# A two-layer Mamba and ternary-FFN kernel: one Strassen sum moved into PSUM, the last step of both layer norms moved from VectorE to ScalarE, and a new priority table

## Chip, cores and metric

The kernel runs on one core of one Trainium2 chip. The metric is the device time of one execution in microseconds (us), as a median of several executions, of the kernel before and of the changed one. Lower is better. The engines are called as in the profile: PE (TensorE matmul), PEld (its weight load), DVE (VectorE), ACT (ScalarE), POOL (GpSimd), SP (SyncE, which issues all the data transfers here).

## What is computed

Input `u` is 2 x 2048 x 512 in fp32. A Mamba-2 layer and a feed-forward layer with ternary weights follow one another, and after each of them the input of the layer is added and the sum is normalised over its 512 columns (post-LN). Cut to what matters here:

```python
def _layernorm(x, eps=1e-05):
    m = jnp.mean(x, axis=-1, keepdims=True)
    v = jnp.var(x, axis=-1, keepdims=True)
    return (x - m) / jnp.sqrt(v + eps)

# attention layer (a selective state space layer), then
x = _layernorm(u + mamba(u))

# feed-forward layer, W_up and W_gate 2048 x 512, W_down 512 x 2048
scale = jnp.mean(jnp.abs(w)) + EPS                       # for each of the three weights
q = jnp.clip(jnp.round(w / scale), -1.0, 1.0) * scale    # ternary weight
h = silu(x @ W_gate.T) * (x @ W_up.T)                    # the ternary weights
y = h @ W_down.T
out = _layernorm(x + y)
```

Which of the two first weights gets the SiLU is a matter of how the kernel stores them and changes nothing below: one half of the Strassen outputs (`c11`, `a2`) goes through SiLU, the other half (`c12`, `c22`) is multiplied by it.

## The kernel before, in words

**Two stages that overlap at one seam.** The first stage is the Mamba layer: 16 groups of 256 positions (`proj`, `steps`, `scan`), each with projections on PE (the lines 616 and 633), a convolution on ACT and DVE (638 and 640), a scan, and an output projection (833) whose operands go through two transposing transfers (824 and 826). While it runs, the weights of the second stage are read twice and made ternary. Results go to `s_scratch` in DRAM. The second stage is the feed-forward layer: 8 blocks of 512 rows (`FSTART`, the loop at 962), and the text below calls them blocks 0 to 7.

**One block of the second stage.** For each of its four chunks of 128 rows: load (`Fs`, `Fu`), add the input (`Fa`, line 970), statistics on DVE (`Fb`, 973 to 975), the power -1/2 on POOL (`Fp`, 977), and then the normalisation itself, `(x - mean) * rstd`, as one DVE instruction over 128x512 (`Fn`, line 978). Then sums of quarters of the block for Strassen's form (`FS`, 991), a split into a high and a low fp16 part (`Fh`, `Fl`, 996 and 997) and a transposing transfer (`FT`, 999). Then eight *pairs* (`pair(p, ...)`, line 920), each for 256 of the 2048 hidden columns. Then, for each chunk, the down projection (`Fd`, 1010, four steps of eight matmuls of 128x512), the residual (`Fr`, 1014), statistics (`Fe`, 1017 to 1019), the power on POOL (`Fq`, 1021), the normalisation on DVE (`Fm`, line 1022) and the store (`Fo`, 1023).

**One pair.** Seven products P1 to P7 (line 932, eight matmuls of 128x256 each) in three PSUM banks, `A`, `Bk` and `Ck`. Bank `A` gathers P1, then P6, then P7, then P4, and after each of the first three ACT copies the sum reached so far to SBUF (`k1` to `p1`, `k2` to `u2`, `k3` to `u3`, all line 936). Bank `Bk` holds P2 alone, and DVE adds the copy to it (`c11` = P2 + `p1`, line 937). Bank `Ck` holds P5, to which DVE adds `u3` (`c22`), then P3 on top of P5, to which DVE adds `u2` (`c12`). ACT takes SiLU of `c11` in place (`a1`, 951) and of bank `A` (`a2`, 952). DVE multiplies (`g`, 956), and `h` on ACT (957) and `l` on DVE (958) split the product into fp16 parts, which are the operands of the down projection.

**Banks.** The kind `fA` has two banks (shared before with `sd`), `fB` two (shared with `tr` and `sd`), `fC` two (shared with `mm`). So a third pair's P2 needs the first pair's `Bk` back, and so on.

**Order.** Nothing is ordered by hand. Each step is recorded with `op(name, engine, cost, function, r=, w=)`. `Order.run` then plays the whole program through with the given costs: each engine takes, of the steps that are ready and have their buffers, the one with the smallest key, and the order found this way is emitted, engine by engine. The keys come from the dictionary `TABLE` (lines 38 to 203), one number per step name, with `name@0` for the first group or block alone. So the order on all five queues follows from the costs and the table. `Var`s read or written in the planner become semaphore waits in the program. 80 filler steps of four matmuls on a matrix of ones (line 572) have no table entry, and so they go where the planner's PE has nothing else to do.

Of the kernel before, what the change touches and what calls it, by code (L numbers as in the profile page):

```python
# [11 lines left out]
F16 = mybir.dt.float16  # L12
AF = mybir.ActivationFunctionType
ALU = mybir.AluOpType
# [24 lines left out]
    "Fh1.3@0": -880.0, "xe4@0": -833.42, "xs3@0": -798.3, "Fr1@0": -749.32, "x1@0": -743.53, "Fk2.4@0": -708.12,  # L39
    "t10@0": -702.07, "FT0@0": -701.5, "Fh0.1@0": -696.72, "x0@0": -647.64, "t00@0": -647.63, "e@0": -617.3, "Fl1.5@0":  # L40
    -611.36, "xg@0": -606.03, "uspw@0": -605.28, "Fl0.4@0": -604.72, "Fl6@0": -595.97, "Fl1.1@0": -595.59, "Fd33@0":
    -577.19, "Fo1@0": -575.43, "Fl0.0@0": -559.34, "Fo2@0": -542.58, "FP6.4@0": -515.99, "Fu0@0": -510.53, "Fg0.6@0":
    -496.82, "Fk1.1@0": -495.69, "Fa1.3@0": -493.84, "Fa2.4@0": -491.28, "Fu1@0": -489.5, "Fa1.0@0": -468.24, "FP4.1@0":
    -464.74, "FT4@0": -443.92, "Fo0@0": -443.36, "t71@0": -441.8, "Fk1.5@0": -434.25, "FP7.3@0": -433.72, "FS5@0":
    -424.07, "Fk3.4@0": -410.98, "sz11@0": -409.89, "t41@0": -408.76, "Fc22.5@0": -403.36, "FS4@0": -400.51, "Fc11.5@0":
    -399.71, "yh.1": -396.1, "B111": -393.2, "wb7ld": -392.43, "xf@0": -390.09, "Fa1.2@0": -389.2, "sg01@0": -387.76,
    "Fk2.1@0": -378.9, "md1.0": -370.41, "Fa1.0": -363.95, "Fl1.7@0": -354.48, "w.1@0": -354.31, "Fk3.2@0": -340.52,
    "Fh0.3@0": -335.11, "Fc22.6@0": -333.55, "Fh1.5@0": -330.02, "Fk3.6@0": -329.97, "sg00": -329.64, "Fk1.2@0":
    -325.88, "Fl0.2@0": -323.01, "Fk3.1@0": -321.43, "Fd12@0": -320.02, "Fe1@0": -318.37, "Fh0.6@0": -316.51, "nA0":
    -314.95, "xe5@0": -313.85, "sz10": -313.05, "Fa1.5@0": -310.03, "FP7.1@0": -305.86, "Fk3.0@0": -305.34, "Fk2.6@0":  # L50
    -304.93, "Fl0.0": -302.95, "yh.0@0": -290.81, "cst@0": -290.24, "ssq.0@0": -289.03, "q2@0": -288.45, "Fc12.4@0":
    -287.51, "q_9@0": -286.63, "Fh0.1": -286.35, "z02@0": -284.82, "x3@0": -283.55, "Fk3.2": -283.16, "xt4@0": -280.75,
    "Fk1.5": -280.01, "Fd10@0": -277.81, "ulo@0": -275.56, "Fh1@0": -272.36, "FP7.5@0": -269.7, "Fd13@0": -269.26,
    "FP3.1@0": -268.96, "Fg0.1@0": -268.88, "wx1hi": -268.5, "Fk1.1": -265.49, "md0.1@0": -265.29, "yg0.1": -259.58,
    "T26": -257.61, "sz11": -256.09, "Fk3.1": -252.55, "wx3sq": -249.32, "Fl0.7@0": -247.92, "cs0@0": -247.82,
    "Fa2.1@0": -245.85, "Fc11.3@0": -245.84, "t72@0": -244.74, "t33": -240.45, "Fk1.7@0": -240.2, "rl@0": -240.04,
    "FP6.1@0": -239.95, "ce.1@0": -239.95, "q1@0": -238.9, "v0": -238.05, "Fd01@0": -237.72, "xec0@0": -236.84,
    "Fa2.2@0": -236.43, "bte@0": -235.45, "FT4": -229.58, "t73@0": -229.2, "xs2": -229.13, "Fq2@0": -229.12, "Fp3@0":
    -228.34, "FP7.5": -227.33, "Fp0@0": -226.27, "Fg1.5": -225.08, "q3@0": -223.61, "t71": -223.59, "t12": -223.14,
    "Fh1.4@0": -223.12, "FP1.1@0": -221.59, "FP3.6@0": -221.11, "cr0": -220.95, "Fg1.5@0": -218.61, "Fh1.2@0": -218.5,  # L60
    "T17": -217.95, "cr1@0": -217.62, "yh.0": -216.95, "Fs2@0": -216.52, "sz02@0": -216.25, "ul@0": -216.02, "s.0@0":
    -215.43, "Fn3@0": -215.09, "xe": -214.89, "B220": -213.53, "Fr1": -210.21, "Fg0.2@0": -206.86, "ec0@0": -204.35,
    "t52": -204.15, "yg1.1@0": -204.07, "cst0": -203.33, "FP7.4@0": -201.23, "wz1rc": -200.8, "usq@0": -200.21,
    "sg00@0": -200.19, "Fe1": -199.59, "T25": -199.49, "szs2": -198.11, "b122": -197.76, "b121": -197.75, "Fd23@0":
    -197.61, "Fk1.2": -197.55, "FP6.6@0": -196.92, "z12@0": -196.48, "wx3rc": -196.43, "Fk3.5@0": -196.29, "xs6":
    -196.28, "q3": -195.54, "t40": -195.35, "sg10@0": -194.31, "wz2ld": -193.93, "xs2@0": -193.52, "st.1@0": -193.33,
    "Fl0.3@0": -192.79, "wb1ld": -192.61, "t42@0": -192.22, "Fa1.5": -192.04, "t82@0": -191.59, "wx1rc": -191.29,
    "m1.0@0": -190.47, "gm.0": -190.01, "yg1.1": -189.77, "o0.1": -189.76, "Fk1.6@0": -189.4, "xt4": -189.35, "xw0.0@0":
    -188.31, "T43": -188.06, "rs.1@0": -187.71, "xe5": -185.77, "wx0sq": -184.8, "wb5lo": -183.47, "t81@0": -182.69,
    "wx8rc": -182.68, "wz0rc": -182.67, "wz0sq": -182.2, "z02": -181.39, "Fc12.2@0": -181.07, "Fl6": -179.08, "t32":  # L70
    -178.42, "xt3": -177.5, "xt5@0": -175.63, "q4": -175.58, "Fk2.1": -174.34, "yd0.0@0": -173.37, "sz12": -172.32,
    "Fg1.7@0": -172.03, "Fc11.4@0": -171.73, "sg11@0": -171.14, "wd0": -168.11, "cs1@0": -166.86, "t80@0": -166.6,
    "cmm@0": -166.05, "wx2mm": -165.65, "Fc22.4@0": -165.51, "xe@0": -165.49, "Fo3@0": -165.02, "Fd03": -164.7, "FT2@0":
    -164.31, "yd1.0@0": -163.73, "x4": -163.52, "wx0mx": -163.51, "dm7": -162.69, "btr": -162.68, "ce.0": -162.14,
    "xt0": -160.74, "Fc12.2": -159.66, "Fc12.4": -159.1, "Fk1.3@0": -157.73, "btr@0": -157.68, "Fh0.3": -157.61, "T36":
    -157.33, "t01@0": -157.03, "Fo2": -156.36, "T15": -155.92, "t01": -155.89, "T20": -155.87, "T21": -155.05, "uspw":
    -155.0, "FP4.2": -154.58, "FT0": -153.73, "xs5@0": -152.56, "T23": -152.33, "wz1pw": -150.53, "Fl0.5": -146.77,
    "yh.1@0": -146.56, "md1.0@0": -146.53, "Fc11.7@0": -145.51, "wx2mx": -141.54, "xt7@0": -140.5, "Fl0.2": -140.44,
    "Fl1.0@0": -137.01, "Fh6@0": -136.3, "q0": -135.1, "wx1mm": -134.74, "Fg1.3@0": -134.09, "wa1ld": -132.88, "wz1sq":
    -131.2, "cs1": -130.62, "m0.0@0": -130.26, "x5@0": -129.87, "dec.1": -128.06, "Fg1.0": -126.87, "FP6.0@0": -126.78,  # L80
    "xe7": -126.54, "wb7hi": -126.27, "t61": -126.26, "Fq0@0": -126.0, "FP5.1@0": -125.85, "wz0mx": -125.2, "tl.0@0":
    -123.56, "FP4.0@0": -122.92, "xe2@0": -121.58, "Fl0.4": -121.56, "Fg0.2": -121.29, "FP4.2@0": -120.92, "x8@0":
    -120.84, "Fh1.0": -120.38, "Fc11.2@0": -120.35, "Fg0.7@0": -119.99, "t03@0": -119.65, "t51@0": -119.23, "t11":
    -119.08, "uh": -119.08, "Fh0@0": -118.27, "Fa2.1": -118.24, "e": -117.06, "Fh0.6": -116.27, "FP3.3": -115.89, "FT3":
    -115.77, "t13@0": -113.43, "Fh2": -112.97, "FP7.1": -112.51, "Fa1.7@0": -112.45, "Fg1.1@0": -112.14, "wx1sq":
    -111.85, "xt6@0": -111.31, "Fd33": -110.87, "yo.1": -109.95, "b120": -109.3, "wa2sq": -108.74, "t00": -108.46,
    "t21": -108.2, "wx8pw": -108.11, "Fk1.7": -107.55, "FP6.2@0": -106.84, "B210": -106.57, "wx8lo": -106.56, "wx8mx":
    -106.52, "t23@0": -105.54, "xt0@0": -105.51, "Fk3.6": -105.47, "wx3mm": -104.71, "Fa1.2": -104.62, "b125": -104.6,
    "uh@0": -104.09, "xs1@0": -103.96, "md1.1": -103.77, "szs0": -103.22, "Fl1@0": -103.22, "xw1.0@0": -103.14, "Fl0.1":
    -103.05, "Fk3.0": -102.44, "stc.0": -102.38, "Fk2.7": -102.36, "yg0.0": -102.3, "wz0lo": -102.2, "q6": -102.18,  # L90
    "t10": -102.16, "gm.1": -101.95, "wz2rc": -101.94, "t02": -101.82, "pw.0": -101.74, "Fk1.0@0": -101.67, "cmm":
    -101.45, "sz10@0": -101.11, "wa4ld": -100.89, "xec0": -99.7, "T14": -99.66, "Fc11.6@0": -99.48, "z00@0": -99.46,
    "wa7ld": -99.04, "wb1hi": -96.71, "cwu0": -96.62, "t63": -96.56, "T22": -96.55, "FP6.1": -95.56, "T11": -95.43,
    "Fa2.3@0": -92.55, "Fk3.4": -91.8, "sz01@0": -91.16, "Fd02@0": -90.79, "Fl0.5@0": -90.31, "Fl5@0": -89.42,
    "Fl1.2@0": -89.28, "Fn1@0": -89.22, "Fg1.4@0": -89.03, "t11@0": -88.61, "Fa1.4@0": -88.6, "cwx1": -88.44, "Fk2.3@0":
# [299 lines left out]
def mamba_ffn_kernel(  # L395
# [45 lines left out]
    with ExitStack() as ph:  # L441
# [478 lines left out]
        def pair(p, xT, hh_, hl_):  # L920
# [17 lines left out]
            prod("P1", 0, B11, A, True, False)  # L938
            copy("k1", p1, A)
            prod("P2", 1, B21, Bk, True, True)  # L940
            add("c11", c11, Bk, p1)
            prod("P6", 5, T2, A, False, False)
            copy("k2", u2, A)
            prod("P5", 4, T1, Ck, True, False)
# [128 lines left out]
```

## Time and profile before

| | us |
|---|---|
| median of 3 executions | 1398.83 (1398.15, 1398.83 and 1402.92) |
| the profiled execution | 1400.29 |
| its span (first to last instruction and transfer) | 1398.6 |
| PE busy | 1373.4 |
| DVE busy | 1141.8 |
| ACT busy | 858.7 |
| POOL busy | 85.8 |

The profile is of one execution. Its busy times are by engine, and "idle before" in a group of instructions is the time that the engine stood still just ahead of them, with what ended it. The mean ns of a matmul in a group is longer than its share of PE's time, since matmuls follow each other before the earlier has ended; how often they start is what counts. The granted TensorE clock of this execution is 0.999.

### The profile page before, as it was taken

The page shows a single profiled execution, that of the slowest core. Times are in us where ns is not written, and L with a number is a line of the kernel's source. Part 1 is how long each engine was busy: PE and PEld are TensorE (multiplying, and loading weights), DVE is VectorE, ACT ScalarE, POOL GpSimd, SP SyncE. Part 2 cuts the span into 40 slices and gives each one's busy share as a digit, 9 for nine tenths or more (in the row PEclk, how much of TensorE's full clock was granted, in tenths as well). Part 3 has the DMA queues.
Part 4 walks back from the last instruction along what each step waited for, and adds up shares of the span by engine and source line. Part 5 has one row for each costly group of instructions (what it writes and reads, how often), then busy time and mean ns, then how long its engine had stood idle before and what let it go on. Part 6 is the DMA issues. An engine that isn't in the chain of part 4 may idle for free.

```text
span 1398.6 us, 26861 instructions
## 1 busy us (share of the span) xinstructions
PE 1373.4 (98%) x10276; PEld 986.8 (71%) x10276; DVE 1141.8 (82%) x2903; ACT 858.7 (61%) x1539; POOL 85.8 (6%) x128
## 2 busy tenths in 40 slices
PE   9999999999999999999999999999999999999997
PEld 8767666766776666767676776868677777768684
DVE  5798898888798999999899766959687786959665
ACT  7778877788776665666677553636454453636351
POOL 1002001000000000000000000000010100000000
PEclk9999999999999999999999999999999999999999
DMA  5354465443444555366649422222222222221100
GB/s 204 108 167 129 114 167 144 145 137 99 133 114 130 135 151 145 86 157 163 140 118 226 129 39 68 53 69 65 57 84 61 76 53 81 49 83 39 46 9 31
DMA packets 186257, 147.04 MB, mean 105 GB/s; under 512 B 133904, under 2 KB 142352, under 8 KB 185872
## 3 DMA queue, kind: packets, MB, share of 16 engines
q1 hardware_dynamic: 186128, 145.33, 39.1%
q8 instruction: 80, 1.31, 0.4%
q14 instruction: 49, 0.40, 0.1%
HBM read 90.63 MB, written 23.20 MB: 81 GB/s over the span
## 4 chain that ended last, share of the span: by engine, by line
PE 49%; ACT 2%; DVE 2%; DMA 1%; issue 0%; POOL 0%; POOLq 0%; ACTq 0%; DVEq 0%
PE sd L932 18%; PE ms L1010 8%; PE mm L932 8%; PE po L1010 8%; PE po L833 2%; PE tr L932 2%; PE mm L616 1%; PE mm L633 1%; DMA th<-yh 1%; PE sd L813 1%; DVE acc L640 0%; DVE cr L806 0%; ACT L743 0%; ACT L644 0%; ACT L745 0%
## 5 line engine op out<-in xcount | busy, mean ns | idle before, releaser
L640 DVE SCALAR_TENSOR_TENSOR acc<-mm,cwu,acc 128x256 f32<-128x256 f32 x432 | 198.4, 474 | 24.1 <-ACT acc L638 22.6
L633 PEld LDWEIGHTS <-wx 128*128 128x128 f16 x1728 | 165.3, 97 | 37.9 <-issue 3.6
L633 PE MATMUL mm<-uh,wx 128*128 128x260 f16 x1152 | 152.5, 274 | 2.4 <-DVE acc L640 0.9
L616 PE MATMUL mm<-wz,uh 128*128 128x344 f16 x768 | 127.7, 309 | 5.1 <-DVE acc L640 3.4
L833 PE MATMUL po<-wo,th 128*128 128x512 f16 x512 | 121.0, 379 | 4.4 <-DMA th<-yh 4.2
L932 PEld LDWEIGHTS <-xt 128*128 128x128 f16 x1024 | 100.2, 98 | 20.4 <-issue 0.9
L957 ACT ACTIVATE sz<-y 128x512 f16<-128x512 f32 x128 | 80.5, 629 | 52.7 <-DVE y L956 40.8
L638 ACT ACTIVATE acc<-mm,cst,cwu 128x256 f32<-128x256 f32 x144 | 79.1, 557 | 53.9 <-PE mm L633 51.9
L932 PEld LDWEIGHTS <-wz 128*128 128x128 f16 x1024 | 100.2, 98 | 16.7
L932 PEld LDWEIGHTS <-wx 128*128 128x128 f16 x1024 | 100.1, 98 | 16.3
L616 PEld LDWEIGHTS <-uh 128*128 128x128 f16 x768 | 74.2, 98 | 41.9 <-issue 4.6
L958 DVE TENSOR_TENSOR cr<-y,sz 128x512 f16<-128x512 f32 x128 | 87.4, 684 | 17.3 <-ACT sz L957 16.5
L936 ACT ACTIVATE ec<-sd 128x512 f32<-128x512 f32 x97 | 57.3, 592 | 70.3 <-DVE y L937 33.3
L1010 PE MATMUL ms<-wo,sz 128*128 128x512 f16 x256 | 97.0, 379 | 0.0
L1010 PE MATMUL ms<-wo,cr 128*128 128x512 f16 x256 | 97.0, 379 | 0.0
L1010 PE MATMUL po<-wo,sz 128*128 128x512 f16 x256 | 97.0, 379 | 0.0
L1010 PE MATMUL po<-wo,cr 128*128 128x512 f16 x256 | 97.0, 379 | 0.0
L833 PEld LDWEIGHTS <-th 128*128 128x128 f16 x512 | 49.2, 98 | 54.6 <-DMA th<-yh 5.0
L633 PE MATMUL mm<-ul,wx 128*128 128x260 f16 x576 | 87.5, 273 | 0.0
L1010 PEld LDWEIGHTS <-cr 128*128 128x128 f16 x512 | 50.1, 98 | 50.5
L1010 PEld LDWEIGHTS <-sz 128*128 128x128 f16 x512 | 50.1, 98 | 50.5
L936 ACT ACTIVATE xw<-sd 128x512 f32<-128x512 f32 x63 | 37.5, 595 | 62.1 <-PE sd L932 33.3
(205 smaller groups left out, 2929.7 us busy)
## 6 DMA issues: line engine op xcount, KB each, us to landing
cr<-cum_scratch SPq DMA_DIRECT2D x32, 512.0 KB, 5.4
uraw<-in_uT_dram SPq DMA_DIRECT2D x16, 520.0 KB, 4.9
ec<-cum_scratch SPq DMA_DIRECT2D x64, 128.0 KB, 5.2
fraw<-in_wupT_dram SPq DMA_DIRECT2D x32, 256.0 KB, 3.1
s_scratch<-s SPq DMA_DIRECT2D x32, 256.0 KB, 2.4
x<-s_scratch SPq DMA_DIRECT2D x32, 256.0 KB, 2.8
fraw<-in_wgateT_dram SPq DMA_DIRECT2D x32, 256.0 KB, 2.9
fraw<-in_wdownT_dram SPq DMA_DIRECT2D x32, 256.0 KB, 3.4
```

Of the source, the lines that this page charges most:

```text
L616: T.matmul(ps[:, :ZC], (uh, ul)[a][:, k, HL + c * P:HL + (c + 1) * P], wz4[b]()[:, j, k, :], start=(n == 0), stop=(n == 11))
L633: T.matmul(ps[:, :TW], wx4[a]()[:, j, k, :], (uh, ul)[b][:, k, :], start=(n == 0), stop=(n == 11))
L638: op(f"t{j}3", "S", act(TG, 2), lambda: S.activation(acc.ap, ps[:, HL:TW], AF.Identity, bias=cb[:, j:j + 1], scale=cwu[:, j, 3:4]), r=[ps, ...
L640: op(f"t{j}{k}", "V", stt(TG), lambda k=k: V.scalar_tensor_tensor(acc.ap, ps[:, 1 + k:1 + k + TG], cwu[:, j, k:k + 1], acc.ap, ALU.mult, A ...
L813: T.matmul(yp[hf][:, i * P:(i + 1) * P], cr[:, h, :], xt[:, c, h, :], start=is_first(g, c), stop=(is_first(g, c) or i == 3))
L833: T.matmul(po.ap, t[:, k, :], wo3[b]()[:, k, :], start=(q == 0 and k == 0), stop=(q == 2 and k == 7))
L932: T.matmul(bank_[:, fi * TG:(fi + 1) * TG], wt[:, kt, f * P:(f + 1) * P], xT[i][:, a, :, kt, :], start=(first and fi == 0 and n == 0), sto ...
L936: copy = lambda nm, t, bank_: o(nm, "S", 0.52, lambda: S.activation(t.ap, bank_.ap, AF.Copy), r=[bank_], w=[t])
L957: o(f"h{t}", "S", 0.54, lambda g_=g_, hv=hv, hh_=hh_: S.activation(hv(hh_), two(g_), AF.Copy), r=[g_], w=[(hh_[p // 2], (p, t))])
L958: o(f"l{t}", "V", tt(512), lambda g_=g_, hv=hv, hh_=hh_, hl_=hl_: V.tensor_tensor(hv(hl_), two(g_), hv(hh_), ALU.subtract), r=[g_, (hh_[p ...
L1010: T.matmul(po.ap, h[qd][:, f, c * P:(c + 1) * P], wd[qd // 2][:, 4 * (qd % 2) + f, :], start=(qd == 0 and f == 0 and a == 0), stop=(qd == ...
```

## The change

Three edits, and a new table.

1. `k1` no longer writes the SBUF buffer `p1` but the bank `Bk` itself. P2 then runs without a start flag, so that it adds to what ACT has put there. The DVE step `c11` is gone, and the SiLU `a1` reads the bank. The buffer `fp1` goes to `fu2` as a third buffer. In block 0 the first two pairs get one more matmul each, `in` (128x512), ahead of `k1`, which starts the bank with any values, so that the later matmuls find the bank's elements written.
2. The normalisations `Fn` and `Fm` go from DVE to ACT, as one Identity activation with two pointer operands (scale and bias). DVE makes the bias, `-mean * rstd`, in a new 128x1 step (`Fz`, `Fy`).
3. P1, P2 and P5 each keep the order of the pairs among themselves (`turn`), and so do the copies `k1` (`turn_k1`).
4. `TABLE` has new numbers for all steps (319 changed lines, left out here). The planner's order of the first stage changes with it.

```diff
-                ("fp1", [on("ec", 0, 0, 2048)]), ("fu2", [on("ec", 1, 0, 2048), on("xw", 0, 0, 2048)]),
+                ("fu2", [on("ec", 1, 0, 2048), on("xw", 0, 0, 2048), on("ec", 0, 0, 2048)]),
...
+        turn = {nm: fixed() for nm in ("P1", "P2", "P5")}
+        turn_k1, oh = fixed(), ones.bitcast(F16)
-        def pair(p, xT, hh_, hl_):
+        def pair(b, p, xT, hh_, hl_):
...
-                o(nm, "PE", 8 * 0.109, mm, r=[xT[i], kf(wt, p)], w=[bank_])
+                o(nm, "PE", 8 * 0.109, mm, r=[xT[i], kf(wt, p)], w=[bank_] + ([turn[nm]] if nm in turn else []))
...
             prod("P1", 0, B11, A, True, False)
-            copy("k1", p1, A)
-            prod("P2", 1, B21, Bk, True, True)
-            add("c11", c11, Bk, p1)
+            if b == 0 and p < 2:
+                o("in", "PE", 0.22, lambda: T.matmul(Bk.ap, oh[:, :P], B11[:, 0, :DM], start=True, stop=True), r=[kf(B11, 0)], w=[Bk])
+            o("k1", "S", 0.52, lambda: S.activation(Bk.ap, A.ap, AF.Copy), r=[A], w=[Bk, turn_k1])
+            prod("P2", 1, B21, Bk, False, True)
...
-            o("a1", "S", silu(512, 1), lambda: S.activation(c11.ap, c11.ap, AF.Silu, scale=facs[:, 0:1]), r=[ksc], w=[c11], table="silu")
+            o("a1", "S", silu(512, 1), lambda: S.activation(c11.ap, Bk.ap, AF.Silu, scale=facs[:, 0:1]), r=[Bk, ksc], w=[c11], table="silu")
...
-                op(f"Fn{c}", "V", 0.46, lambda c=c, x1=x1, mv=mv, rs=rs: V.tensor_scalar(x1[:, c, :], x1[:, c, :], mv[:, 0:1], rs[:, 1:2], ALU.subtract, ALU.mult),
+                op(f"Fz{c}", "V", 0.08, lambda mv=mv, rs=rs: V.scalar_tensor_tensor(mv[:, 0:1], mv[:, 0:1], -1.0, rs[:, 1:2], ALU.mult, ALU.mult), r=[rs], w=[mv])
+                op(f"Fn{c}", "S", act(DM, 2), lambda c=c, x1=x1, mv=mv, rs=rs: S.activation(x1[:, c, :], x1[:, c, :], AF.Identity, bias=mv[:, 0:1], scale=rs[:, 1:2]),
                    r=[mv, rs], w=[(x1, c)])
...
-                op(f"Fm{c}", "V", 0.46, lambda r=r, mv=mv, rs=rs: V.tensor_scalar(r.ap, r.ap, mv[:, 0:1], rs[:, 1:2], ALU.subtract, ALU.mult), r=[mv, rs], w=[r])
+                op(f"Fy{c}", "V", 0.08, lambda mv=mv, rs=rs: V.scalar_tensor_tensor(mv[:, 0:1], mv[:, 0:1], -1.0, rs[:, 1:2], ALU.mult, ALU.mult), r=[rs], w=[mv])
+                op(f"Fm{c}", "S", act(DM, 2), lambda r=r, mv=mv, rs=rs: S.activation(r.ap, r.ap, AF.Identity, bias=mv[:, 0:1], scale=rs[:, 1:2]), r=[mv, rs], w=[r])
```

## The prediction

> **What bounds the kernel now.** First the page's top, then busy time in four stretches, then three blocks of the second stage by themselves, then PE's own waits, then the end. The first fence is the page's head.
>
> ```profile
> span 1398.6 us, 26861 instructions
> ...
> PE 1373.4 (98%) x10276; PEld 986.8 (71%) x10276; DVE 1141.8 (82%) x2903; ACT 858.7 (61%) x1539; POOL 85.8 (6%) x128
> ...
> PEclk9999999999999999999999999999999999999999
> ```
>
> PE is busy for 1373.4 of 1398.6 us at the full clock, so 25.2 us are all that a change which leaves the products alone can win. The next view, busy time by stretch (each column an engine, in brackets its instructions), tells where they lie.
>
> ```profile
> 0.00:100.00 100.00, 94.14 (x773) 75.28 (x774) 72.71 (x229) 76.15 (x142) 9.97 (x21) 1.00 0.51 159
> 100.00:800.00 700.00, 688.12 (x5094) 480.06 (x5092) 627.03 (x1892) 499.21 (x925) 40.54 (x51) 1.00 0.53 139
> 800.00:1392.00 592.00, 591.10 (x4413) 431.48 (x4411) 439.34 (x779) 283.30 (x474) 34.23 (x54) 1.00 0.22 56
> 1392.00:1398.60 6.60, 0.00 (x0) 0.00 (x0) 2.75 (x7) 0.00 (x0) 1.10 (x2) 0.85 0.21 79
> ```
>
> PE stands for 5.9 us in the first 100, 11.9 us in the rest of the first stage, 0.9 us in nearly all of the second stage, 6.6 us after the last matmul. The second stage is the one that edits 1 and 2 touch. Three of its blocks, in the same columns:
>
> ```profile
> 899.40:976.00 76.60, 76.60 (x579) 56.40 (x578) 59.46 (x109) 37.81 (x65) 5.08 (x8) 1.00 0.25 66
> 976.00:1052.60 76.60, 76.60 (x579) 56.42 (x577) 59.56 (x108) 37.87 (x65) 5.08 (x8) 1.00 0.25 66
> 1052.60:1129.20 76.60, 76.60 (x579) 56.42 (x578) 59.47 (x108) 37.80 (x64) 5.08 (x8) 1.00 0.25 66
> ```
>
> Each lasts 76.60 us and PE is busy for all of it. A block's matmuls alone make 8 pairs x 7 products x 0.873 us (eight matmuls that start every 0.109 us) + 16 down steps x 1.727 = 76.5 us. So a steady block can't get shorter by anything done to DVE (78% busy) or ACT (49%). PE's waits, longest first, show what the first stage's idle time waits for:
>
> ```profile
> PE po L833 <- DMA th<-yh: 4.2, 3, 1.6
> PE mm L616 <- DVE acc L640: 3.4, 4, 1.9
> PE tr L648 <- ACT xt L650: 2.0, 5, 0.7
> PE mm L616 <- DVE v L621: 1.5, 1, 1.5
> ```
>
> The largest is the transposing transfer `th`, three times, 1.2 to 1.6 us each. Last, the end, in order of time:
>
> ```profile
> 1391.97 0.75 DVE L1014 SCALAR_TENSOR_TENSOR s<-po,facs,x 128x512 f32<-128x512 f32 x1
> ...
> 1392.77 0.55 DVE L1022 TENSOR_SCALAR junk<-junk,mv,lnr 128x512 f32<-128x512 f32 x1
> 1393.23 0.69 DVE L1017 BATCH_NORM_STATS2 bst<-s 128x6 f32<-128x512 f32 x1
> ...
> 1395.05 0.55 DVE L1022 TENSOR_SCALAR s<-s,mv,lnr 128x512 f32<-128x512 f32 x1 [0.73 <-POOL lnr L1021]
> 1395.63 0.33 SPq L1023 DMA_DIRECT2D out_dram<-s  x1
> ```
>
> The last chunk's statistics stand behind the normalisation of the chunk before (`junk`), on DVE's queue.
>
> **The change, part by part.**
>
> *The sum `c11`.* 64 DVE adds of 0.686 us (line 937) go: 43.9 us of DVE, 5.5 in a block. On the path: nothing, since PE covers them. `k1` stays one ACT copy. No row has ACT writing PSUM. Reading PSUM instead of SBUF takes 35 ns off (592 against 627 ns, lines 936 and 996), so I bound the write to PSUM by 557 and 627 ns and take 592; over 64 copies that is 2.2 us of ACT either way. `a1` now reads PSUM as `a2` does: 685 for 718 ns, 2.1 us of ACT less.
>
> What is new is a wait: P2 now waits for `k1`, and with P2 everything behind it in PE's queue. I counted the PE work that stands between them in the order the changed program was emitted in. After P1, `k1` needs 0.16 (the last matmul's tail, 273 less 109 ns), 0.03 of hand-over, 0.59 and about 0.06 back: 0.84 us. In a steady block P1 to P2 has 1.75 us of other products once (pair 0) and 5.2 to 20.9 us in the other seven. P6 waited for `k1` before and still does. Short covers of 1.73 to 1.75 us, over P1-P2, P1-P6, P6-P7 and P7-P4, are 10 in a block before and 12 after, and the 10 cost nothing in the blocks shown. So I take 0, with 0.9 us of margin at each; if that is gone, each overrun costs its own length (a rival below). At the seam, pair 0 of block 0 has only one scan step of 0.9 us between P1 and P2: up to 0.1 us.
>
> The two `in` matmuls are PE work: 2 x 0.216 (a 512-wide matmul starts every 0.216 us at line 1010) = +0.43.
>
> The Trainium skill speaks against the seed: "PSUM — Partial Sum Buffer", "Summary: rules for kernel authors", says that a sum seeded by ACT or DVE must be seeded with 0, as these engines do not set the bits by which a matmul adds, and its section "The four PSUM rules" would send any other seed through PE. No row here shows those bits. By that advice a seed per pair would be 62 more `in` matmuls, +13.4 us; the diff issues two, so the sum has two.
>
> *The normalisations.* 32 `Fn` of 539 and 32 `Fm` of 544 ns leave DVE (34.7 us), and 64 steps on 128x1 come (166 ns, from the 128x16 step of line 698; bounds 153, line 975, and 222, line 621): 10.6 us. On ACT 64 activations with two pointers: without pointers 627 ns (line 996), and two pointers add 182 (line 638 with two takes 557 at 128x256, line 650 without 375): 0.81 us, so 51.8 us; bounds 0.63 (pointers free) and 0.90 (the one-pointer SiLU of line 951, 718 ns, and 182 more). A steady block then has DVE 59.5 - 5.5 - 4.3 + 1.3 = 51.0 and ACT 37.8 - 0.3 + 6.5 = 44.0 of 76.6 us. Both lie under PE. DVE gets 67.9 us lighter in all, and in the second stage no wait of PE's is there to get shorter. Behind `Fn` on ACT stand the splits `Fh` and copies, behind `Fo`, which now waits for ACT, SP's loads for the next block; both are covered by the 33 us of ACT's idle time in a block and by a block's lead of those loads, so 0, and at most 0.81 each on the last chunk, counted below. Of the 64, the eight `Fn` of the first two blocks fall into the first stage, 6.5 us on an ACT that is busy for 499 of 700 us. The third buffer `fu2` and the `turn` orders issue no instruction: 0.
>
> The Trainium skill says the same against the move: "ScalarE: Activation LUTs", "Rules for kernel authors", puts add and multiply on VectorE. The rows agree in sign, 0.54 on DVE against an estimated 0.81 on ACT. If ACT set the pace the move would cost 64 x 0.27 = 17 us; at 57% of a block it doesn't.
>
> *The end.* `Fm` on ACT is 0.81 for 0.55, behind a step of 0.17 and two hand-overs of 0.06 on the last chunk: +0.55. The last statistics now wait for a step of 0.17 instead of one of 0.55: -0.4. Together +0.15. In block 7 PE waits 0.74 us for `k3` (its longest wait for line 936): before, P4 of pair 7 stands directly behind P7; in the new order two other products stand between: -0.74.
>
> *The table.* It moves the first stage, where 17.8 us of idle PE lie. Filler steps and products open in nearly the same order in both programs (15, 6, 7 and 3 fillers between the same four small matmuls), so I leave the first 100 us alone: 0, bounds -5.9 (its whole idle time) and +5.9. ACT loads its tables 76 times for 74, 2 x 1.28 us on an engine 71% busy there: 0. For `th` I counted again. From the scan's last product to the output projection a chunk needs 0.68 (815) + 1.24 (820) + 0.15 + 0.73 (822) + 1.14 (823) + 3.1 (median issue to landing of `th`) and six hand-overs of about 0.1: 7.7 us. PE work standing in that place is under 9.5 us for 6 of 32 chunks before (least 8.6) and for 10 after (least 8.2). Such a transfer took 5.4 and 7.4 us where PE waited for it, so covers this thin are what it overruns. In proportion, 4.2 x 10/6 = 7.0, that is +2.8; bounds -4.2 (none is late) and +9.8 (all ten late by 1.4 us, the mean of the three, is 14.0 for 4.2). The other waits after 100 us, 11.9 - 4.2 = 7.7 us, I leave as they are, with half of them, 3.9, either way.
>
> *Sum.* 1398.6 + 0.43 + 0.15 - 0.74 + 2.8 = 1401.2 us of span. The profiled execution took 1400.29, its median sibling 1398.83; a change of +2.6 on the median is **1401.4**.
>
> **Rivals.** *The new order closes gaps (faster).* If half of the 17.8 us goes, 1398.83 - 8.9 - 0.2 = 1389.7. For it: the 25.2 us are all idle time that an order makes. Against it: the thinner covers for `th`.
>
> *ACT's queue in the pairs (slower).* Place: a copy that PE waits for in the next two products. Point: more than 0.9 us of other work ahead of it, which one normalisation of 0.81 doesn't make and two do, by 0.7. 64 normalisations stand among these copies; if a third meets a short cover, 21 x 0.7 = 15 us: 1398.83 + 15 = 1414. For it: ACT's 12 short covers a block and 16% more work. Against: 57% load and no such stall before.
>
> *The first stage opens (slower).* Its waits after 100 us double: +11.9, 1411. For it: a new order for all five queues, DVE 90% busy there (627 of 700 us). Against: its sequence on PE is nearly the old one.
>
> *The edits do nothing* is my forecast's core: the adds and normalisations they take from DVE end no wait of PE's.
>
> **How the numbers follow.** A measurement here tells about 0.5%, 7 us, from no change: 1391.8 to 1405.8. Forecast, within that: 0.55. Gaps close: 0.17. ACT's queue: 0.12. First stage opens: 0.16. So faster 0.17, same 0.55, slower 0.28. The range reaches towards both sides' cases, 1391 to 1412.
>
> **What would show it.** Steady blocks of 76.6 us with PE full, DVE near 51 and ACT near 44 us in each, confirm edits 1 and 2; a longer block with PE waiting for an ACT copy at the product line is the ACT rival. Waits of the output projection for `th` near 7 us in all confirm the table's term; under 3 would make me wrong on the fast side. Idle PE between 0 and 800 us below 9 us is the first rival, above 25 the last.

## The result, and the profile after

The changed kernel takes **1395.52 us** (median of 10, 1392.94 to 1397.21) against 1399.63 us for the kernel before in the same session (median of 10, 1396.62 to 1404.96): a ratio of 0.9967, 95% interval 0.9956 to 0.9977. A second comparison, the first experiment below, gives 0.9975 (0.9965 to 0.9986). So it is faster by a quarter to a third of one per cent, 3.5 to 4.6 us. The forecast was 1401.4 us and no difference that can be told; the time lies inside the range, 1391 to 1412, and inside the band of half a per cent, but on the other side of the time before.

The profiled execution took 1392.94 us, the fastest of the ten. First the head of its page.

```profile
span 1391.2 us, 26837 instructions
...
PE 1374.3 (99%) x10278; PEld 986.6 (71%) x10278; DVE 1083.2 (78%) x2839; ACT 901.8 (65%) x1605; POOL 80.9 (6%) x128
...
PEclk9999999999999999999999999999999999999999
```

PE does 0.9 us more than before (1373.4) and stands for 16.9 us where it stood for 25.2. DVE has 58.6 us less to do and ACT 43.1 more. Busy time by stretch tells where PE's idle time went (the columns are length, PE, PEld, DVE, ACT, POOL, granted clock, DMA share and GB/s).

```profile
0.00:100.00 100.00, 97.34 (x791) 76.73 (x792) 74.72 (x236) 83.48 (x151) 9.94 (x21) 1.00 0.52 165
100.00:800.00 700.00, 692.86 (x5137) 484.01 (x5135) 626.20 (x1889) 505.29 (x934) 36.12 (x51) 1.00 0.52 138
800.00:1384.20 584.20, 584.14 (x4355) 425.81 (x4353) 380.11 (x709) 311.42 (x519) 33.70 (x54) 1.00 0.23 57
1384.20:1391.20 7.00, 0.00 (x0) 0.00 (x0) 2.14 (x8) 1.62 (x2) 1.10 (x2) 0.71 0.20 76
899.40:976.00 76.60, 76.60 (x578) 56.37 (x577) 52.27 (x99) 42.63 (x71) 5.07 (x8) 1.00 0.28 66
```

Idle PE in the first 100 us fell from 5.9 to 2.7 us, from 100 to 800 us from 11.9 to 7.1, after that from 0.9 to 0.1; the end after the last matmul grew by 0.3 us. So nearly all that was won was won in the first stage, which the two edits of arithmetic hardly touch. A steady block, the last row, still lasts 76.60 us with PE full. PE's waits, longest first:

```profile
PE mm L616 <- ACT sz L623: 1.6, 4, 0.6
PE mm L633 <- DVE acc L640: 1.4, 4, 0.4
PE tr L648 <- ACT xt L650: 1.2, 2, 0.7
PE po L572 <- DVE ones L418: 1.1, 1, 1.1
PE tr L648 <- ACT xc L644: 1.0, 2, 0.8
PE po L833 <- DMA th<-yh: 0.8, 1, 0.8
```

The longest wait of before, 4.2 us in three for the transposing transfer `th`, is down to one of 0.8 us. The one of 3.4 us for `acc` at line 616 and the one of 1.5 us for `v` are gone; line 616 now waits for `sz`, 1.6 us in four. No wait of the second stage is among the longest any more. Last, the end, in order of time:

```profile
1384.37 0.75 DVE L1019 SCALAR_TENSOR_TENSOR s<-po,facs,x 128x512 f32<-128x512 f32 x1
...
1385.13 0.16 DVE L1027 SCALAR_TENSOR_TENSOR mv<-mv,lnr 128x1 f32<-128x1 f32 x1
1385.21 0.69 DVE L1022 BATCH_NORM_STATS2 bst<-s 128x6 f32<-128x512 f32 x1
1385.33 0.81 ACT L1028 ACTIVATE junk<-junk,mv,lnr 128x512 f32<-128x512 f32 x1 [11.17 <-DVE mv L1027]
...
1387.51 0.81 ACT L1028 ACTIVATE s<-s,mv,lnr 128x512 f32<-128x512 f32 x1 [1.37 <-DVE mv L1027]
1388.35 0.33 SPq L1029 DMA_DIRECT2D out_dram<-s  x1
```

The last statistics now stand behind a step of 0.16 us instead of one of 0.55, and the last normalisation takes 0.81 us on ACT, as was worked out from two pointers' price.

### The profile page after: what moved, and what is told of

Same layout as the page of the kernel before. It is cut to its first block, busy times and chain, and to the rows that moved or that the text cites. A ratio compares the mean times of both kernels' runs of the same rounds, so it can differ in the third digit from the quotient of the medians.

```text
span 1391.2 us, 26837 instructions
## 1 busy us (share of the span) xinstructions
PE 1374.3 (99%) x10278; PEld 986.6 (71%) x10278; DVE 1083.2 (78%) x2839; ACT 901.8 (65%) x1605; POOL 80.9 (6%) x128
## 4 chain that ended last, share of the span: by engine, by line
PE 69%; DVE 14%; ACT 10%; DMA 4%; issue 2%; POOL 0%; SPq 0%; POOLq 0%; ACTq 0%; DVEq 0%
PE sd L935 18%; PE mm L935 8%; PE ms L1015 8%; PE po L1015 8%; PE mm L616 7%; PE mm L633 6%; PE po L833 6%; DVE acc L640 4%; PE tr L935 2%; PE sd L813 2%; DVE cr L724 1%; PE sd L776 1%; DVE y L815 1%; PE tr L648 1%; DVE yl L825 1%
## 5 line engine op out<-in xcount | busy, mean ns | idle before, releaser
L640 DVE SCALAR_TENSOR_TENSOR acc<-mm,cwu,acc 128x256 f32<-128x256 f32 x432 | 201.6, 476 | 16.4 <-ACT acc L638 14.3
L961 ACT ACTIVATE sz<-y 128x512 f16<-128x512 f32 x128 | 79.1, 626 | 56.7 <-DVE y L960 54.6
L623 ACT ACTIVATE sz<-mm,szs 128x344 f32<-128x344 f32 (+1 forms) x96 | 51.8, 539 | 37.3 <-PE mm L616 33.8
L935 PE MATMUL sd<-fraw,wx 128*128 128x256 f16 x576 | 73.8, 273 | 0.0
```

Source lines behind the costliest of these rows:

```text
L623: op(f"sz{c}{j}", "S", act(w, 1), lambda: S.activation(d["sz"][c][:, j * ZC:j * ZC + w], ps[:, :w], AF.Silu, scale=szs[:, j:j + 1]), r=[ps ...
L640: op(f"t{j}{k}", "V", stt(TG), lambda k=k: V.scalar_tensor_tensor(acc.ap, ps[:, 1 + k:1 + k + TG], cwu[:, j, k:k + 1], acc.ap, ALU.mult, A ...
L935: T.matmul(bank_[:, fi * TG:(fi + 1) * TG], wt[:, kt, f * P:(f + 1) * P], xT[i][:, a, :, kt, :], start=(first and fi == 0 and n == 0), sto ...
L961: o(f"h{t}", "S", 0.54, lambda g_=g_, hv=hv, hh_=hh_: S.activation(hv(hh_), two(g_), AF.Copy), r=[g_], w=[(hh_[p // 2], (p, t))])
```

## The experiments

Two things differ between the kernels: the edits of arithmetic, and the order of all five queues that the new table makes. Eleven runs took them apart. In most of them the planner was replaced by a fixed list of steps, so that one kernel's code ran in the other's order; with its own list each kernel's queues come out as the planner makes them. "The change" is 1396.14 us below, its median of the first experiment, and differences between kernels are made from the ratios to the kernel before, which ran beside each of them (1398.8 to 1399.9 us).

**The change again.** No edit.

> The changed kernel once more, to have its time beside the three others and a second trace of it. Both theories expect 1395.5 +- 1 us (ratio 0.997 to the kernel before), PE idle about 10 us before 800 us and blocks of 76.6 us. If the idle time before 800 us of this second trace differs from the first trace's 9.8 us by more than 3 us, single traces are too noisy to place the gain.

Measured: 1396.14 us, 0.9975 (0.9965 to 0.9986). Idle PE is 3.4 us in the first 100 and 8.6 us from 100 to 800 in its profile (span 1394.4), 2.2 us more than in the first profile of the same program. That is the scatter of such a number; this second profile, nearer to the median, is the one to compare with.

**The two stages' orders crossed.** Steps of the first stage in one kernel's order, everything else, code too, from the other kernel.

```diff
 # new edits, old first stage: the changed kernel
-order of the first stage's steps: as changed
+order of the first stage's steps: as before
 # old edits, new first stage: the kernel before
-order of the first stage's steps: as before
+order of the first stage's steps: as changed
```

> The changed code with its own order in the second stage, and on every queue the first stage's steps in the order of the kernel before. Theory 1 (the new order of the first stage makes the gain): about 1399.3 us, ratio 0.9995 to 1.0005, that is the second stage's edits alone come to -0.2 us (two seed matmuls +0.4, end +0.3, the 0.7 us wait in the last block gone). Theory 2 (the edits make it, by a lighter DVE at the seam and in the second stage): 1395.5 us, ratio 0.997.

> The code of the kernel before with its own order in the second stage, and on every queue the first stage's steps in the changed kernel's order. Theory 1 (order of the first stage): about 1395.7 us, ratio 0.997, PE idle near 10 us before 800 us. Theory 2 (the edits): about 1399.6 us, ratio 1.000.

Measured: 1413.78 us, 1.0098 (1.0081 to 1.0116), and 1412.11 us, 1.0094 (1.0077 to 1.0111). Both crossings cost some 13 us over the kernel before, so neither theory holds as it was put. Much of PE's added idle time lies at the seam: between 690 and 800 us PE stands for 7.4 and 11.4 us (4.0 before, 1.9 in the change), in the second kernel 4.7 us of it in one wait for `v`. Up to 690 us the first stage's order shows even so: 16.4 us of idle PE with the old one and 11.3 with the new one (13.7 before, 10.1 in the change). The second stage's loads, normalisations and splits stand on DVE's, ACT's and SP's queues among the first stage's last groups, so it may be that the two stages' orders are made for each other there; no run separates this. How a whole table would do with only one of its stages changed can't be read from such a crossing.

**The new opening alone.** The kernel before, with the steps planned in the first 95 us in the changed order.

```diff
-order of the steps planned before 95 us: as before
+order of the steps planned before 95 us: as changed
```

> The code and order of the kernel before, but the steps that are planned in the first 95 us stand in the changed kernel's order. In the two traces PE's idle time fell from 5.9 to 2.7 us in the first 100 us and from 11.9 to 7.1 us up to 800. Theory 1a (the opening gives its part): -3 us, ratio 0.998. Rival 1b (the gain lies in the waits after 100 us, three for the transposing transfer among them): ratio 1.000. Theory 2: 1.000.

Measured: 1401.66 us, 1.001 (1.0001 to 1.002). Idle PE in the first 100 us is 3.5 us, 2.4 less than before, and 14.7 us from 100 to 800, 2.8 more. One trace can't place differences of this size: the other three kernels with the old opening show 3.7, 3.9 and 4.5 us there, and the kernels with the new one 2.7 to 3.8. So the opening itself seems worth about 1 us of idle time, and the time shows no gain from it.

**One edit at a time in each order.** Four kernels. The first three run in the changed order, with every step that both programs have in the same place on every queue.

```diff
 # old edits, new order; also "sum on DVE" without the last two lines
-            o("k1", "S", 0.52, lambda: S.activation(Bk.ap, A.ap, AF.Copy), r=[A], w=[Bk, turn_k1])
-            prod("P2", 1, B21, Bk, False, True)
+            copy("k1", p1, A)
+            prod("P2", 1, B21, Bk, True, True)
+            add("c11", c11, Bk, p1)
...
-                Fz, Fy on DVE (128x1), then Fn, Fm on ACT (128x512)
+                Fn, Fm on DVE (128x512) in the places of Fz, Fy
 # "norm on DVE": the last two lines alone
 # old order, norm on ACT: the kernel before with the last two lines turned round
```

> The sum c11 is again a DVE add and both normalisations end on DVE, as in the kernel before; every step that both kernels have stands in the changed kernel's order on all five queues (each c11 just behind the product P2 of its pair, the normalisations at the places of the small steps that replaced them). One tile is no longer shared, so that this order needs no wait the changed kernel doesn't have. Theory A (the order as a whole makes the gain, the two edits of arithmetic nothing): about 1396 us, 0.9975 of the kernel before, idle PE of 10 to 13 us before 800 us. Theory B (the lighter DVE makes it: 68 us less work there): 1400 us or more, ratio 1.000 or above, idle PE near the 17.8 us of the kernel before.

> The changed kernel, with the last step of both normalisations back on DVE at the places of the small steps; the sum in PSUM and the order stay. Theory A: 1396 us, 0.9975, and the end after the last matmul 0.1 to 0.3 us shorter. Theory B: between 1396 and 1400, since 24 of the 68 us of DVE are given back, eight of the 64 steps before the second stage.

> The changed kernel with the sum c11 back on DVE (43.9 us of DVE, 5.5 in a block, just behind the product P2 of its pair) and the normalisations left on ACT; order on all five queues as changed. It is the fourth corner of new order x two edits. Theory C (the new order's blocks are cut so close that each edit's lighter DVE queue is needed, and the two add up): 1403.1 for the kernel without the norm edit and 1414.7 without both make 11.6 us for the sum, so about 1407.5, ratio 1.006, with PE idle 0.6 to 0.9 us in a steady block. Rival (only the 1.2 us wait that the sum and a normalisation make together behind each other counts; one of them alone fits): 1400 or less.

> The kernel before with one edit: the last step of both normalisations on ACT, in the places where DVE did it; its order stays. Theory A: 1399.9 us, 1.000 (0.1 to 0.3 us more at the end). Theory B: below the kernel before, 1398 or less, idle PE before 800 us below 16 us.

Measured:

| order | sum `c11` | normalisation | us | ratio (95%) | idle PE 0-720 | 720-800 | 800-1384 |
|---|---|---|---|---|---|---|---|
| old | DVE | DVE | 1399.63 | 1 | 15.2 | 2.5 | 0.8 |
| old | DVE | ACT | 1407.47 | 1.0067 (1.0049-1.0085) | 16.3 | 3.0 | 3.4 |
| new | PSUM | ACT | 1396.14 | 0.9975 (0.9965-0.9986) | 10.1 | 1.9 | 0.0 |
| new | PSUM | DVE | 1403.09 | 1.0034 (1.0022-1.0045) | 10.8 | 1.8 | 3.7 |
| new | DVE | ACT | 1410.39 | 1.0077 (1.0062-1.0093) | 11.0 | 5.1 | 5.3 |
| new | DVE | DVE | 1414.7 | 1.0116 (1.0097-1.0135) | 10.7 | 5.1 | 9.6 |

The columns of idle time answer both theories. In the first 720 us the order decides: 10.1 to 11.0 us with the new one, whatever the edits, and 15.2 to 16.3 with the old one. There theory A was right. After that the edits decide, and there it was wrong: put back into the new order, the normalisation on DVE costs 8 us (1.0034 less 0.9975), the sum on DVE 14 us, both 20 us. Alone they cost 8 and 14, together 20, so they nearly add up, as theory C had it, though its 1407.5 us was 3 too low. And the one edit tried alone in the old order, the normalisations on ACT, makes the kernel before 9 us slower. The sum in PSUM alone and both edits together were not run in the old order. So an order made for one program need not suit another, not even one with less work on its busier engine.

Idle time is a part of these costs only. Against the change's second profile idle PE ahead of the end grows by 4.3, 9.4 and 13.4 us (normalisation, sum, both on DVE), and PE's busy time by 3.1, 3.9 and 6.3 us for the same matmuls or two fewer. In the second stage the two costs add up: a steady block lasts 77.6 us with either edit taken back and 78.6 with both, against 76.6. Much of what the sum on DVE costs beyond that lies at the seam, 5.1 us of idle PE for 1.9 and a slow stretch after it (last section).

Where this happens can be seen in a steady block of the kernel with both old edits in the new order. The timeline there (start, us; for PE the idle time before and its releaser):

```profile
958.62 0.68 DVE L883 TENSOR_TENSOR y<-mm,xw 128x512 f32<-128x512 f32 x1
959.22 0.54 DVE L924 TENSOR_SCALAR x<-x,mv,lnr 128x512 f32<-128x512 f32 x1
959.68 1.28 DVE L904 TENSOR_TENSOR cr<-y,sz 128x512 f16<-128x512 f32 x2
960.88 0.68 DVE L883 TENSOR_TENSOR y<-mm,state 128x512 f32<-128x512 f32 x1
961.48 0.68 DVE L916 TENSOR_TENSOR x<-x,us 128x512 f32<-128x512 f32 x1
...
961.62 1.03 PE L878 MATMUL mm<-uh,wz 128*128 128x256 f16 x8 [1.19 <-DVE y L883]
```

PE wants the bank `mm`, which the add of line 883 (`c12` or `c22`; with the lines shifted, line 937 of the kernel before) has to read first. On DVE's queue that add stands behind a normalisation (line 924) and two splits (904), and so PE waits 1.19 us, in the same place in block after block. DVE is busy for 58.1 us in a stretch of 76.6 us there. In the kernel before it is busy for 59.5, and PE never waits. A share of busy time tells nothing about such a place; what stands ahead of the one step that PE needs does.

**More work for ACT.** The changed kernel with one more copy ahead of every normalisation.

```diff
-op(f"Fm{c}", "S", ..., lambda ...: S.activation(r.ap, r.ap, AF.Identity, bias=mv[:, 0:1], scale=rs[:, 1:2]), ...)
+op(f"Fm{c}", "S", ..., lambda ...: (S.activation(r.ap, r.ap, AF.Copy), S.activation(r.ap, r.ap, AF.Identity, bias=mv[:, 0:1], scale=rs[:, 1:2])), ...)
```

> The changed kernel with an ACT copy of 128x512 in place ahead of every normalisation: 64 copies of about 0.63 us, 40 us more of ACT, 5 us in each block of the second stage, the order unchanged. Theory A (PE sets the time, ACT at 56% of a block has room): 1396 to 1397, blocks of 76.6 us, 0.6 us more at the end. Rival (ACT's queue in the pairs, as in the prediction): a third of the 64 met by a short cover at about 0.6 us each, 13 us, 1409.

Measured: 1401.78 us, 1.002 (1.0009 to 1.0031), 6 us over the change: between the two expectations. Idle PE before 800 us is 11.8 us, as in the change. A steady block lasts 77.3 us and has 0.25 us of idle PE, 0.15 of it where P2 waits for `k1`, which stands behind the copy, a normalisation and a SiLU on ACT; after 800 us it is 1.5 us in all. PE's busy time is 2.2 us longer, and the end is as long as before. The profiled execution was the fastest of twelve and its span only 3.7 us longer, so the rest of the 6 us is not placed. So ACT, at 56% of a block, has no room for 5 us more in this order, though the loss is less than a sixth of the 40 us added.

**The three late `th` covered.** The kernel before; on PE's queue alone, in the chunks where PE waited for `th` (`o0.0@10` are the eight matmuls of group 10's first chunk on `th`, `o1` the eight after them; `x`, `z`, `xt`, `gps` are projections, transposes and sums of later groups):

```diff
-yd0.1@10  o0.0@10  x0@11  z00@11  o1.0@10
+yd0.1@10  x0@11  z00@11  o0.0@10  o1.0@10
-x4@15  o0.0@13  z12@15  o1.0@13
+x4@15  z12@15  o0.0@13  o1.0@13
-x0@15  o0.0@14  xt6@15  gps.1@15  o1.0@14
+x0@15  xt6@15  gps.1@15  o0.0@14  o1.0@14
```

> The kernel before with one thing moved on PE's queue: in the three chunks where the output projection waited for the transposing transfer (1.22, 1.36 and 1.63 us), its eight matmuls stand behind the next one or two products instead of ahead of them. Theory A (a wait taken away in the first stage is won): waits for th below 1 us, idle PE from 100 to 800 us 11.9 - 3.5 = about 8.4, 1395.5 us, ratio 0.9975. Rival (given back: DVE, 90% busy there, sets the pace, as with the new opening alone, where 2.4 us won came back as 2.8 lost): waits for th below 1 us as well, but idle PE from 100 to 800 us 11 or more, 1398.5 to 1399.5, ratio 1.000.

Measured: 1399.29 us, 0.9999 (0.9989 to 1.001). The waits for `th` went from 4.2 to 1.0 us, and the time stayed. PE's waits from 650 to 720 us show what took one's place. Before:

```profile
PE po L833 <- DMA th<-yh: 1.4, 1, 1.4
PE tr L648 <- ACT xt L650: 0.4, 1, 0.4
PE sd L776 <- DVE state L798: 0.2, 1, 0.2
```

With `th` covered (line 561 is line 616 of the kernel before, 593 is 648, 721 is 776):

```profile
PE mm L561 <- DVE acc L585: 1.3, 1, 1.3
PE tr L593 <- ACT xt L595: 0.4, 1, 0.4
PE sd L721 <- DVE state L743: 0.2, 1, 0.2
```

The wait of 1.4 us for the transfer became one of 1.3 us for DVE's convolution. From 100 to 800 us idle PE is 10.6 us where it was 11.9, so of 3.2 us of waits taken away 1.3 is left as less idle time in this profile, and nothing in the time that 11 executions could tell. The rival was right on the time; on idle PE the run lies between the two. Some of the idle time is scatter: in the first 720 us this profile has 12.3 us for 15.2, though its order up to group 10 is the old one, and 1.4 us of that difference lies in the opening.

**A seed for every pair.** The changed kernel with its `in` matmul in all 64 pairs.

```diff
-            if b == 0 and p < 2:
+            if True:
                 o("in", "PE", 0.22, lambda: T.matmul(Bk.ap, oh[:, :P], B11[:, 0, :DM], start=True, stop=True), ...)
```

> The changed kernel with an `in` matmul of 0.216 us ahead of every k1, 64 for 2, as the rule on seeded sums would have it; order unchanged. Theory A (PE sets the pace of the second stage, so PE work adds up): 62 x 0.216 = 13.4 us, 1409.4, blocks of 78.3 us with no idle PE. Rival (the added matmuls give ACT and DVE time, or wait for their bank): below 1406 or above 1413.

Measured: 1416.53 us, 1.012 (1.0101 to 1.0139), 20 us over the change. PE is busy for 1391.3 us, 15.9 more than in the change's second profile, for 13.4 us of matmuls. A steady block shows the rest:

```profile
959.20:1035.80 76.60, 76.05 (x564) 54.89 (x562) 49.92 (x97) 41.08 (x69) 5.08 (x8) 1.00 0.26 66
```

PE stands for 0.55 us in it: an `in` needs its bank free sooner than `k1` did, and the waits listed are for the SiLU `a1` that reads it (0.6 us at the longest). A block lasts 79.1 us where the matmuls alone would make 78.3. The rival above 1413 was right: added matmuls cost their own length and, here, half as much again.

## Why the prediction was right and wrong

**The step that failed is the table's term, +2.8 us for `th`** ("In proportion, 4.2 x 10/6 = 7.0, that is +2.8"). The waits for `th` went from 4.2 to 0.8 and 0.9 us in the two profiles, so the sign was wrong. Of the 32 transfers, four took over 4 us from issue to landing before (4.4 to 7.4) and eight after (4.2 to 6.2), so late transfers became more frequent, much as the thinner covers suggested. But for seven of the eight PE had other work for long enough: it came to their first product 4.2 to 9.5 us after the issue, when the transfer had landed (once by 0.05 us), and waited for one instead of three. Over all 32 transfers this lead is no longer than before (median 6.0 and 6.1 us, 6.5 before). So what changed is which transfers are late, and there is luck in it. The prediction named this sign itself: waits for `th` "under 3 would make me wrong on the fast side". A count of thin covers in proportion takes the late transfers to be spread evenly over the chunks, and they aren't: before, those of 5.9 and 7.4 us were issued 4.9 and 2.5 us after the first of two loads of `cr` (512 KB each), the one of 5.4 us 1.3 us after another transposing transfer. And the term was wrong in kind: where a wait was taken away by itself the time didn't follow it, so the shorter waits for `th` don't explain the gain by themselves either. The other waits after 100 us, left at 7.7 us, came out at 6.3 and 7.7.

**The opening, left at 0 with bounds of 5.9 either way**, is the other part. It went to 2.7 and 3.4 us. Most of this was never the order's: the three other kernels with the old order throughout the opening show 3.7 to 4.5 us there and not 5.9. And alone it wins nothing. What the new order is worth shows only in the whole: 10.1 instead of 15.2 us of idle PE in the first 720 us, some 5 us, near to the 4.2 by which the spans differ (1398.6 and 1394.4). Against the forecast span of 1401.2 us, the waits for `th` came out 6.1 us lower and the opening 2.5, and PE's busy time, which grew by 2.0 us where 0.43 was set down, takes back 1.6: near to the 6.8 us that the second profile lies below it. The first rival, "gaps close", named the mechanism and over-sized it: 8.9 us were set down for it.

**Which of the new order's many moves makes these 5 us is open.** The two that were tried alone, the opening and the covers of `th`, make no gain that can be measured.

**The two edits end no wait of PE's: right for the order before, wrong as a rule.** "On the path: nothing, since PE covers them" held in the changed kernel: blocks of 76.60 us, PE full. It does not follow that the edits are idle. In the new order they are worth 20 us. The prediction read DVE's 78% and 49% for ACT as room, and the five kernels above with 47 to 76% on these engines in a block and a standing PE show that such a share doesn't tell.

**ACT's queue in the pairs, the second rival,** did not come in the changed kernel. Its mechanism, two normalisations ahead of a step that PE needs, came in a relative: with the normalisations on ACT in the old order, the SiLU `a2`, which frees the bank that the next P1 wants, stands behind two normalisations and two splits (2.6 us), and PE waits 0.44 us for it in a steady block. The prediction's list of short covers doesn't have this wait. With one more copy of 0.63 us in the new order PE waits 0.25 us in a block, 0.15 of it for `k1`, the wait that the edit of the sum made.

**The small terms.** The end was put at +0.15 and measures +0.3. The wait of 0.74 us in block 7 is gone, as expected. The two `in` were +0.43; PE's busy time grew by 0.9 in one profile and 2.0 in the other. `k1` writes PSUM in 0.584 us (taken: 0.592), `a1` takes 0.683 (0.685), the small steps 0.152 to 0.157 (0.166), the normalisations 0.804 to 0.814 (0.81). DVE is 58.6 us lighter, not 67.9, and ACT 43.1 heavier, not 49.7: in a block 52.3 us and 42.6 where 51.0 and 44.0 were expected. Each engine's instructions overlap their neighbours' ends (a DVE add of 0.68 us starts 0.60 us after the one before, as at 960.88 and 961.48 above), so a mean duration, taken 64 times, is more than its removal frees. Summed instruction by instruction the durations changed by -65.7 and +49.9 us, close to the forecast.

**The Trainium skill's two rules, against runs.** "PSUM — Partial Sum Buffer", "Summary: rules for kernel authors", asks for a seed of 0 where ACT or DVE writes it. The kernel's other seeds rest on one starting matmul in each bank. Starting every pair with a matmul, still with ACT's seed behind it, was put at 13.4 us and costs 20, the eleventh kernel; a seed written by PE itself was not run. "ScalarE: Activation LUTs", "Rules for kernel authors", puts add and multiply on VectorE. The single instruction agrees, 0.81 us on ACT against 0.54 on DVE, and the kernel differs: in the new order the normalisations on DVE cost 8 us more, in the old order those on ACT cost 9 more.

## What to carry to other kernels

Where PE is full and everything else runs beside it, price an edit together with the order that it runs in: the same two edits were worth 20 us in one order, and one of them alone cost 9 us in the other. Don't add up waits as if each were won back when it goes; take one away in a run of its own and see whether the next takes its place. And read the room of a second engine from what stands ahead of the one step that PE needs next, not from its busy share.

## What the runs showed of the hardware

**A stop of 3 us costs TensorE clock afterwards.** In the kernel with old edits in the new first stage, PE waits 4.7 us from 699.3 on. Stretches of 5 us around it (the third column from the right is the granted clock):

```profile
700.00:705.00 5.00, 1.06 (x6) 0.73 (x6) 4.89 (x11) 2.46 (x5) 0.00 (x0) 0.73 0.09 31
705.00:710.00 5.00, 5.00 (x24) 3.04 (x23) 3.49 (x12) 1.24 (x3) 0.00 (x0) 0.59 0.35 79
710.00:715.00 5.00, 5.00 (x38) 3.21 (x37) 4.33 (x16) 4.65 (x9) 0.00 (x0) 1.00 0.44 65
```

After the stop the clock is at 0.59 and 24 matmuls start in 5 us; in the next 5 us it is 1.00 and 38 start. The two kernels with the sum on DVE and the new order have the same at the seam, and here the price can be read from the second one's list of PE's work:

```profile
784.30 1.86 PE L880 MATMUL sd<-uh,xt 128*128 128x256 f16 x8 [3.02 <-ACT state L884]
785.96 2.43 PE L781 MATMUL po<-wo,th 128*128 128x512 f16 x8
788.23 1.04 PE L880 MATMUL mm<-uh,wz 128*128 128x256 f16 x8
```

From 784.30 to 788.23 are 3.93 us for two groups that take 8 x 0.109 + 8 x 0.216 = 2.60 us at full rate. So the wait of 3.02 us cost 1.3 us on top (1.7 in its sibling, after 2.93 us). After the longest waits in two kernels without such a stop, 2.4 us (new edits, old first stage) and 1.9 us (the kernel before), no stretch of 5 us shows a clock below 1.00. The Trainium skill, "TensorE: Matmul & The Clock Gate", "What's actually happening", has the array at half its clock after an idle window of about 3.4 us; stops of 2.9 and 3.0 us were enough here, the only ones of that length.

**PE's busy time differs for the same matmuls.** PE is busy for 1375.4 us in the change and 1381.7 in its sibling with both old edits, which has fewer matmuls by two. The slow stretch explains 1.7 us of the 6.3; what makes the other 4.6 is open. How long PE stands doesn't set it alone: the kernel before stands for 25.2 us, the change for 19.0, and it is busy for 2.0 us less.
